# Attention stage of a two-layer kernel: row loads in a hand-written order, the edges' rows moved forward, mixing in four column groups

## The chip, the cores and the metric

One core of one Trainium2 chip runs the whole program. The metric is the time of one execution on the device, in microseconds (us); lower is better. Times are given as the median of several runs, and one more execution was recorded by the hardware profiler. TensorE is called PE here, VectorE DVE, ScalarE ACT, GpSimd POOL and SyncE SP; SPq is SP's queue of transfers.

## The reference, cut to what matters

Two layers on a tensor x of 4 images, 192 channels and 128 x 128 pixels, in float32. The stage in question is the attention of the first:

```
qkv = dwconv3x3(conv1x1(x, w_qkv), w_dw)
q, k, v, l = jnp.split(qkv, 4, axis=1)
q, k, v = (heads(q), heads(k), heads(v))          # b, 8 heads, 24 channels, 128*128
q = q / jnp.maximum(jnp.linalg.norm(q, axis=-1, keepdims=True), EPS)
k = k / jnp.maximum(jnp.linalg.norm(k, axis=-1, keepdims=True), EPS)
attn = jax.nn.softmax(jnp.einsum('bhcn,bhdn->bhcd', q, k) * temperature[None], axis=-1)
out = jnp.einsum('bhcd,bhdn->bhcn', attn, v).reshape(b, c, h, w)
...
out = conv1x1(L + out + x, w_proj) + L
```

The attention is over channels: each head's result is a 24 x 24 matrix for each image. L is a small gate from the mean of l. The second layer adds a depthwise convolution to this output and makes a local attention over 3 x 3 neighbours with dilations 1, 2 and 3.

## The kernel before

The program has three stages.

**Projection** (`project`). It multiplies x with w_qkv and stores the rows of q and k, still without their 3 x 3 convolution, to `qk_dram`, laid out by image row, channel, image and column. It convolves v and stores it. A planner orders the instructions of all engines by costs and due times (`Schedule`, `Stage`); the change doesn't touch it.

**Channel attention** (`channel_attention`, the stage of the change). It goes through 8 heads. A head has 24 channels of q and 24 of k; these 48 channels n are taken in 6 tiles of 8 (in the text, tile 1 to tile 6 of a head; in the code a tile is numbered from 0 over all heads). For each tile:

- a transfer `few` (L705) loads the taps of the vertical filters, and POOL spreads them into a banded matrix `band` (L730, L732): 4 times one large copy and two small ones,
- 16 transfers (L719) load the rows into a buffer u of 2 MB: 32 image rows of two channels each, to 32 partitions. Three buffers take turns: `lent`, which is memory of the last stage, and two of `u_p`,
- PE convolves (`convolve`, L740) with 32 x 32 blocks of `band`, on all sixteen 32 x 32 parts of its array. Each of the 8 channels takes 12 products. The order is such that three channels are in work at a time. ACT copies each result out of PSUM (L749), and DVE gathers its statistics (L751).

Image rows are cut into four strips of 32 rows, so the rows at the three strip edges lack a neighbour. They are mended apart: `cut_loaded` (L775) loads 4 image rows around an edge in 4 transfers (q or k, two halves of the channels), each of 48 partitions with 2 KB; `cut_convolved` (L791) makes their products, `cut_kept` copies them out on ACT, `cut_turned` (L808) transposes them, and `cut_squares` adds them to the squares of the norms.

`products` is the end of a head: the products of edges 0 and 1, then for each of 4 images 128 products `gram` of q with k (L847), between them the turning of an edge and, after the first image, the products of edge 2. `finish` makes the softmax; it is called in pieces while the next head is convolved. `mix` multiplies the 24 x 24 matrices of a head with 24 rows of w_proj (L927) and writes the result into `mix1` and `mix2` by transfers (L931, L934); it is called in two pieces of two images each from the next head's `products`, and its transfers and that of `wph` (L920) are issued by ACT.

**Second pass**: it multiplies x and v with `mix1` and `mix2` and does the second layer. PE, DVE and POOL are busy in it nearly all the time.

What sets the order in the attention: PE's instructions stand as they are written (`tc.manual_schedule`). Those of SP, ACT, DVE and POOL are put in order by the framework's scheduler, from the data they wait for. [...] A transfer that SP or ACT issues also waits until the one eight places before it has landed, since eight semaphores take turns for both queues.

Of the kernel before, what the change touches and what calls it, by code (L numbers as in the profile page):

```python
# [7 lines left out]
F32 = mybir.dt.float32  # L8
# [318 lines left out]
def channel_attention_then_dilated_attention(ctx: ExitStack, tc: tile.TileContext, d, out: bass.AP):  # L327
# [23 lines left out]
    with ExitStack() as early:  # L351
        band_p, u_p = (early.enter_context(tc.tile_pool(name=n, bufs=k)) for n, k in (("pab", 1), ("pau", 2)))
        gate_w = early.enter_context(tc.tile_pool(name="p1g", bufs=1))
        gate_p = early.enter_context(tc.tile_pool(name="p1s", bufs=2))
        sums = []
        for p in range(B // 2):
            xsum = gate_p.tile([128, 3, NB], F32, tag="xsum", name=f"xsum{p}")
            xcol = gate_p.tile([128, 3, 2, H], F32, tag="xcol", name=f"xcol{p}")
            xrow = gate_p.tile([128, 3, 3], F32, tag="xrow", name=f"xrow{p}")
            nc.gpsimd.memset(xrow, 0.0)  # L360
            sums.append((xsum, xcol, xrow))
        later = {}
# [14 lines left out]
        channel_attention(tc, d, load, qk_dram, mix1, mix2, band_p, u_p, gate_p, lent, gates)  # L377
        w2 = {n: later[n] for n in SECOND}
# [291 lines left out]

def channel_attention(tc, d, load, qk_dram, mix1, mix2, band_p, u_p, gate_p, lent, gates):

# [6 lines left out]
    with ExitStack() as ctx:  # L679
# [3 lines left out]
        cut_p = ctx.enter_context(tc.tile_pool(name="pac", bufs=1))  # L683
        few_p = ctx.enter_context(tc.tile_pool(name="pax", bufs=2))
        st = ctx.enter_context(tc.tile_pool(name="pas", bufs=1))
# [3 lines left out]

        bands = [band_p.tile([128, 4, 2, 3, STRIP], F32, tag=f"band{k}", name=f"band{k}") for k in range(2)]  # L690
# [9 lines left out]

        def loaded(hd, which, j):

            c0 = which * C + hd * CH0 + j
            few = few_p.tile([STRIP, 4, 2, 3, STRIP], F32, tag="few", name=f"few{which}_{hd}_{j}")
# [4 lines left out]
            )  # L709
            turn = 3 * (2 * hd + which) + j // 2  # L710
            if turn % 3 == 0:
                u = lent.rearrange("p (e c w) -> p e c w", e=4, c=2)
            else:
                u = u_p.tile([128, 4, 2, B * W], F32, tag="u", name=f"u{which}_{hd}_{j}")
            for e in range(4):
                first = c0 + e * (CH0 // 4)
                for r in range(4):
# [4 lines left out]
                    )  # L722
            if hd and len(bands) == 2:
                for k in range(2):
                    bands.append(gate_p.tile([128, 4, 2, 3, STRIP], F32, tag="xcol", name=f"band{2 + k}"))
                    nc.gpsimd.memset(bands[-1], 0.0)
            band = bands[turn % len(bands)]
            for i in range(4):
                group = slice(i * STRIP, (i + 1) * STRIP)
                nc.gpsimd.tensor_copy(band[group, :, :, :, 1 : STRIP - 1], few[:, :, :, :, 1 : STRIP - 1])  # L730
                for e, m in ((i, 0), ((i + 1) % 4, STRIP - 1)):
                    nc.gpsimd.tensor_copy(band[group, e, :, :, m : m + 1], few[:, e, :, :, m : m + 1])  # L732
            return band, u

# [33 lines left out]

        def cut_loaded(hd, edge, queue):
            u = cut_p.tile([128, 2, B * W], F32, tag=f"u{edge % 2}", name=f"cut{hd}_{edge}")  # L770
            first = (edge + 1) * STRIP - 2
            for which in range(2):
                for h in range(2):
                    c0 = which * C + hd * CH0 + h * (CH0 // 2)
                    queue.dma_start(  # L775
                        u[h * G : h * G + 2 * CH0, which],
                        qk_dram[first : first + 4, c0 : c0 + CH0 // 2].rearrange("r c b w -> r c (b w)"),
                    )
            return u
# [45 lines left out]
        def products(hd, q, sq, k, sk, us, taps):  # L825
            gram = ps_c.tile([128, B, W], F32, tag="pc", name=f"gram{hd}")[:, :, : 2 * CH0]
            cuts, two = [], 2 * CH0
            pcut = cut_convolved(hd, (0, 1), us, taps)
            us[2] = cut_loaded(hd, 2, nc.scalar)
            s_cut = cut_kept(hd, 0, pcut)  # L830
            for b in range(B):
                for v in range(W // 4):
                    if v == W // 8 and b < 2 and mixes:
                        next(mixes[0], None)
                        if b:
                            mixes.pop()
                    if (b, v) == (3, W // 8):
# [48 lines left out]
            by_image = lambda a: a.rearrange("p (b c) -> p b c", b=B)  # L886
            nc.vector.tensor_copy(logits[:, :, hd % 2, :], by_image(sm[:, : B * CH0]))
            nc.vector.tensor_copy(nk[:, :, hd % 2, :], by_image(sm[:, B * CH0 : 2 * B * CH0]))
            nc.vector.tensor_copy(nq[:, :, hd % 2], sm[:, 2 * B * CH0 : EXTRA])

        def finish(hd):


            rows, norm_q, norm_k = logits[:, :, hd % 2, :], nq[:, :, hd % 2], nk[:, :, hd % 2, :]
            wide = lambda a: a.unsqueeze(2).to_broadcast([CH0, B, CH0])
# [16 lines left out]
            nc.vector.tensor_mul(rows, rows, wide(tot))  # L912
            mixes.append(mix(hd))
            next(mixes[-1])

        def mix(hd):

            low = min(max(128 - hd * CH0, 0), CH0)
            wph = fin.tile([CH0, C], F32, tag="wph", name=f"wph{hd}")
            nc.scalar.dma_start(wph, d["wph"][:, hd, :])  # L920
            yield
            for b in range(0, B, 2):
                mixed = fin.tile([CH0, 2, C], F32, tag="mixed", name=f"mixed{hd}_{b}")
                pm = ps_s.tile([128, SM], F32, tag="sm", name=f"pm{hd}_{b}")
                two = pm[:CH0, : 2 * C].rearrange("p (h o) -> p h o", h=2)
                for e in range(2):
                    nc.tensor.matmul(two[:, e, :], logits[:, b + e, hd % 2, :], wph, start=True, stop=True)  # L927
                nc.vector.tensor_copy(mixed, two)
                for e in range(2):
                    if low:  # L930
                        nc.scalar.dma_start(mix1[b + e][hd * CH0 : hd * CH0 + low], mixed[:low, e, :])  # L931
                    if low < CH0:
                        at = G + hd * CH0 + low - 128
                        nc.scalar.dma_start(mix2[b + e][at : at + CH0 - low], mixed[low:, e, :])  # L934
                yield

        pending, mixes = [gate(ps_s) for gate in gates], []

        def step():
            while pending:  # L940
                try:
                    return next(pending[0])
                except StopIteration:
                    pending.pop(0)

        def head(hd):

# [4 lines left out]
            order = sorted((0.75 * n + k, n, dx) for n in range(2 * CH0) for k, dx in enumerate((1, 0, 2)))  # L952
            sources, pcs, sums = {}, {}, []
            for _, n, dx in order:
                which, j, e = n // CH0, n % CH0 // 4, n % 4
                if dx == 1:
                    if n % 8 == 0:
                        sources[n // 8] = loaded(hd, which, j)
                    if n == 40:
                        taps = cut_taps(hd)  # L960
                        us = {edge: cut_loaded(hd, edge, nc.sync) for edge in range(2)}
                    pcs[n] = ps_c.tile([128, B, W], F32, tag="pc", name=f"pc{hd}_{n}")
                convolve(*sources[n // 8], e, j % 2, pcs[n], dx)
# [12 lines left out]
        )  # L976
        with tc.manual_schedule(engines={mybir.EngineType.PE}):
            for hd in range(HEADS0):
                head(hd)
            while pending:  # L980
                step()
            for left in mixes:
                for _ in left:
                    pass

# [643 lines left out]
```

## Time and profile before

| | |
|---|---|
| median of 3 runs | 4297.07 us (4279.99 to 4302.99) |
| profiled execution, its own time | 4289.94 us |
| its span, first to last instruction | 4288.2 us |
| granted clock of PE, mean | 0.972 |
| busy share of PE, DVE, POOL, ACT | 96%, 89%, 79%, 61% |
| first product of the attention, start of the last stage's products | 841.25 us, 1499.57 us |

The profile is one execution. Its page gives the busy time of each engine, the span in 40 slices with a digit for the busy share in tenths and the granted clock of PE (9 is 0.9 or more), and groups of instructions by line: `line engine operation out<-in shape xcount | busy us, mean ns | idle before it, and what ended that`. A timeline row is `start us, us, engine line operation xcount [idle before <- what ended it]`. A row of a stretch gives the stretch, its length, the busy time and number of instructions of PE, PEld (weight loads), DVE, ACT and POOL, then PE's granted clock, the mean busy share of the 16 DMA engines and GB/s. Matmuls overlap, so that PE counts as busy while it works at a low rate.

### The profile page before, as it was taken

What the parts mean: (1) busy time and instruction counts of PE and PEld (TensorE: products, weight loads), DVE (VectorE), ACT (ScalarE), POOL (GpSimd) and SP (SyncE); (2) the same over time, 40 slices, a digit from 0 to 9 for tenths busy, and PEclk for the clock granted to TensorE, in tenths of its full rate; (3) what the DMA queues carried; (4) which work ended last, traced back from release to release, by engine and by line L of the source; (5) the groups of instructions that cost most, each with busy time, mean ns of one, the idle gap of its engine ahead of it and who ended that gap; (6) DMA issues with size and microseconds to landing.
All of it is one profiled execution on the core that took longest, in us unless ns stands there. A gap on an engine that the chain in (4) does not pass through costs nothing.

```text
span 4288.2 us, 79574 instructions
## 1 busy us (share of the span) xinstructions
PE 4115.1 (96%) x28064; PEld 1642.4 (38%) x28064; DVE 3820.6 (89%) x5588; ACT 2627.7 (61%) x4882; POOL 3388.9 (79%) x3411
## 2 busy tenths in 40 slices
PE   8999999799999978999999999999999999999996
PEld 3333333365665522333333333333333333333331
DVE  6999999875576548999999999999999999999996
ACT  6999999743344365565656656556655656656531
POOL 6888888732233226999999999999999999999998
PEclk9999999898899989999999999999999999999997
DMA  8888898666576577656666666655655556555521
GB/s 239 265 270 256 266 287 284 201 184 171 163 191 188 150 160 124 132 125 133 132 127 134 125 132 122 135 129 125 135 126 132 123 135 131 130 132 127 117 47 32
DMA packets 482907, 677.16 MB, mean 158 GB/s; under 512 B 143060, under 2 KB 318304, under 8 KB 482508
## 3 DMA queue, kind: packets, MB, share of 16 engines
q1 hardware_dynamic: 441468, 501.43, 41.6%
q0 software_dynamic: 37888, 166.74, 21.1%
q8 instruction: 223, 3.65, 0.4%
q10 hardware_dynamic: 3152, 3.89, 0.3%
q14 instruction: 176, 1.44, 0.1%
HBM read 278.08 MB, written 201.33 MB: 112 GB/s over the span
## 4 chain that ended last, share of the span: by engine, by line
PE 68%; DVE 14%; DMA 5%; issue 4%; POOL 3%; SPq 3%; ACT 1%; ACTq 0%; POOLq 0%; DVEq 0%
PE sc L1281 9%; PE ex L1403 8%; PE ph L1048 7%; PE pu L427 6%; PE pkv L1202 5%; PE pc L740 5%; DVE term L1409 4%; PE pkv L1205 4%; PE q L1262 4%; PE q L1259 4%; PE pu L432 3%; DVE prod L1270 3%; PE gram L847 2%; POOL acc L1412 2%; SPq L719 2%
## 5 line engine op out<-in xcount | busy, mean ns | idle before, releaser
L1412 POOL TENSOR_TENSOR acc<-acc,term 128x512 f32<-128x512 f32 x1536 | 2034.8, 1330 | 142.1 <-DVE term L1409 55.3
L1409 DVE TENSOR_TENSOR term<-ex,vring 128x512 f32<-128x512 f32 (+2 forms) x1596 | 995.4, 659 | 57.0 <-PE ex L1403 43.4
L1270 DVE TENSOR_TENSOR prod<-q,kring 128x1536 f32<-128x1536 f32 (+1 forms) x600 | 1004.6, 1683 | 20.2 <-PE q L1259 8.8
L504 POOL TENSOR_TENSOR v_True<-v_True,side 128x512 f32<-128x512 f32 (+1 forms) x512 | 643.3, 1268 | 125.8 <-ACT side L493 95.6
L1403 PE MATMUL ex<-e_sb,spread 108*128 108x512 bf16 x1728 | 567.2, 387 | 49.7 <-DVE term L1409 32.4
L481 DVE SCALAR_TENSOR_TENSOR pa<-vboth,dwv,pa 128x1024 f32<-128x1024 f32 (+1 forms) x448 | 574.2, 1282 | 42.2 <-ACT pa L474 14.4
L1215 ACT COPY kring<-pkv 64x512 f32<-64x512 f32 x384 | 223.2, 581 | 417.4 <-PE pkv L1205 411.8
L730 POOL COPY band<-few 32x720 f32<-32x720 f32 x192 | 151.1, 787 | 396.2 <-DMA few<-in_bands 336.1
L1100 DVE SCALAR_TENSOR_TENSOR pa<-hboth,posw,pa 128x1024 f32<-128x1024 f32 (+1 forms) x320 | 407.5, 1273 | 37.0 <-ACT pa L1088 18.1
L1281 PE MATMUL sc<-prod,pick 128*32 128x512 f32 x3456 | 428.8, 598 | 1.7 <-DVE prod L1270 1.7
L1403 PEld LDWEIGHTS <-spread 108*128 108x128 bf16 x1728 | 133.2, 97 | 660.6 <-issue 638.4
L1428 ACT COPY o<-po 128x512 f32<-128x512 f32 x192 | 106.2, 588 | 442.6 <-PE po L1425 237.3
L1048 PE MATMUL ph<-lent,mix 128*64 128x512 f32 (+1 forms) x1024 | 374.1, 596 | 0.6 <-DMA mix<-mixed 0.6
L1202 PE MATMUL pkv<-y,wkv 128*128 128x512 f32 x768 | 364.3, 596 | 9.8 <-DMA y<-moved 9.6
L427 PE MATMUL pu<-xt,wx 128*128 128x512 f32 x768 | 357.2, 608 | 16.8 <-ACT vboth L463 8.9
L493 ACT ACTIVATE side<-ring,dwv 128x512 f32<-128x512 f32 (+1 forms) x512 | 347.8, 724 | 30.1 <-POOL v_True L504 26.3
L1132 ACT ACTIVATE side<-hring,posw 128x512 f32<-128x512 f32 (+1 forms) x512 | 340.9, 710 | 13.0 <-DMA side<-side 11.1
L751 DVE BATCH_NORM_STATS2 stats<-conv 128x6 f32<-128x128 f32 x1536 | 304.4, 274 | 29.2 <-ACT conv L749 26.6
L749 ACT COPY conv<-pc 128x512 f32<-128x512 f32 x384 | 228.7, 616 | 127.6 <-PE pc L740 120.5
L740 PE MATMUL pc<-u,band 32*32 32x508 f32 (+1 forms) x6144 | 276.0, 595 | 4.1 <-DMA u<-qk_dram 1.9
L1215 ACT COPY vring<-pkv 64x512 f32<-64x512 f32 x384 | 223.8, 583 | 45.5 <-PE pkv L1205 32.5
L427 PEld LDWEIGHTS pu<-xt,wx 128*128 128x128 f32 x768 | 142.3, 192 | 222.4 <-issue 121.5
(170 smaller groups left out, 6340.4 us busy)
## 6 DMA issues: line engine op xcount, KB each, us to landing
qk_dram<-us SPq DMA_DIRECT2D x192, 512.0 KB
side<-side POOLq DMA_DIRECT2D x124, 768.0 KB, 7.2
u<-qk_dram SPq DMA_DIRECT2D x512, 128.0 KB
xt<-in_x SPq DMA_DIRECT2D x64, 512.0 KB
v_dram<-v_False SPq DMA_DIRECT2D x64, 512.0 KB
lent<-qk_dram SPq DMA_DIRECT2D x256, 128.0 KB
lent<-in_x SPq DMA_DIRECT2D x128, 256.0 KB
lent<-v_dram SPq DMA_DIRECT2D x128, 256.0 KB
```

The costliest lines, as they stand in the source:

```text
L427: mm(pu, wx[:, mt * 128 : (mt + 1) * 128], tiles["xt", n][:, im, :], start=True, stop=False)
L481: nc.vector.scalar_tensor_tensor(by_row(to[:, o : o + length]), by_row(vboth[:, at : at + length, :, t % 3 : t % 3 + W]), dwv[:, 0, t : t ...
L504: nc.gpsimd.tensor_add(v[:, rows, :], v[:, rows, :], z[:, rows, :])
L740: nc.tensor.matmul(pc[r * STRIP : (r + 1) * STRIP, :, to], band[at, e, c, dx, :], u[at, e, c, :].rearrange("p (b w) -> p b w", w=W)[:, :, of],
L1048: mm(to, w[:, cols], tiles["xv", n, j, im], start=j == 0, stop=j == 2)
L1202: mm(rows3(tile_of("pc", key)), w, tiles["y", n, im], start=True, stop=False)
L1215: nc.scalar.copy(rows[HALVES[im], :, pad : pad + W], rows3(tiles["pkv", n, pair, im])[HALVES[e]])
L1270: nc.vector.tensor_mul(to[:, :, px].rearrange("p t (r w) -> p t r w", w=W), q.unsqueeze(1).to_broadcast([128, 3, *q.shape[1:]]), three,)
L1281: mm(sc[quad * 32 : (quad + 1) * 32, :], pick[:, QR - 4 * row : QR - 4 * row + 32], tiles["prod", n, k // NT, k % NT // 3][:, k % 3, :], s ...
L1403: mm(rows3(tile_of("ex", ("ex", n, g, t))), spread[:, t, :], e_sb, start=True, stop=True)
L1409: nc.vector.tensor_mul(rows3(to[:, px]), rows3(ex[:, px]), win)
L1412: nc.gpsimd.tensor_add(tiles["acc", n, g], tiles["acc", n, g], tiles.pop(("term", n, g, t)))
```

## The change

It has five parts, all in `channel_attention`.

1. SP's order is now written by hand too. `load_rows(t)` loads tile t of the 48 tiles of all heads. Three are loaded ahead of the first head; from then on, tile t + 3 is loaded once tile t has been convolved. All of a tile's 16 transfers and its taps stand together.
2. There are three band matrices, one for each buffer, where there were two in the first head and four in the others; the taps `few` have one buffer instead of two.
3. The taps of the edges and the rows of all three edges (12 transfers) are loaded right after tile 5 of the same head has been asked for (n == 15), all by SP, into three buffers. Before, SP loaded edges 0 and 1 and ACT loaded edge 2 after the products of the first two.
4. The products of edge 2 come right after those of edges 0 and 1, ahead of the first image's `gram`.
5. `mix` is one piece for all 4 images: four products side by side in four column groups of PE, one copy by DVE. The 24 columns of the softmax's matrix are padded to 32 with zeros for that. Its transfers are issued by POOL, and `wph` is loaded by SP.

```
-        bands = [... for k in range(2)]
+        bands = [... for k in range(3)]
...
-        logits = fin.tile([CH0, B, 2, CH0], F32, tag="logits", name="logits")
+        logits = fin.tile([CH0, B, 2, STRIP], F32, tag="logits", name="logits")
+        nc.gpsimd.memset(logits, 0.0)
...
-        def loaded(hd, which, j):
+        def load_rows(t):
+            if t >= 6 * HEADS0:
+                return
+            hd, which, j = t // 6, t // 3 % 2, t % 3 * 2
...
-            band = bands[turn % len(bands)]
+            band = bands[t % 3]
...
-            return band, u
+            sources[t] = band, u
...
-            u = cut_p.tile([128, 2, B * W], F32, tag=f"u{edge % 2}", name=f"cut{hd}_{edge}")
+            u = cut_p.tile([128, 2, B * W], F32, tag=f"u{edge}", name=f"cut{hd}_{edge}")
...
-            pcut = cut_convolved(hd, (0, 1), us, taps)
-            us[2] = cut_loaded(hd, 2, nc.scalar)
+            pcut = {**cut_convolved(hd, (0, 1), us, taps), **cut_convolved(hd, (2,), us, taps)}
...
-                    if v == W // 8 and b < 2 and mixes:
-                        next(mixes[0], None)
-                        if b:
-                            mixes.pop()
+                    if (b, v) == (1, W // 8) and mixes:
+                        mixes.pop()()
...
-                if b == 0:
-                    pcut.update(cut_convolved(hd, (2,), us, taps))
...
+            pm = ps_s.tile([128, SM], F32, tag="sm", name=f"pm{hd}")[:, :C]
+            for b in range(B):
+                mine = slice(b * STRIP, (b + 1) * STRIP)
+                nc.tensor.matmul(pm[mine], logits[:, b, hd % 2, :], wph[hd], start=True, stop=True)
+            mixed = fin.tile([128, C], F32, tag="mixed", name=f"mixed{hd}")
+            nc.vector.tensor_copy(mixed, pm)
+            for b in range(B):
+                first = b * STRIP
+                if low:
+                    nc.gpsimd.dma_start(mix1[b][hd * CH0 : hd * CH0 + low], mixed[first : first + low])
...
+        def load_mixing(hd):
+            wph[hd] = fin.tile([CH0, C], F32, tag="wph", name=f"wph{hd}")
+            nc.sync.dma_start(wph[hd], d["wph"][:, hd, :])
...
-                    if n % 8 == 0:
-                        sources[n // 8] = loaded(hd, which, j)
-                    if n == 40:
-                        taps = cut_taps(hd)
-                        us = {edge: cut_loaded(hd, edge, nc.sync) for edge in range(2)}
...
                 evicted(fulls[which], stats[which], e * (CH0 // 4) + j, pcs.pop(n))
+                if n % 8 == 7:
+                    load_rows(6 * hd + n // 8 + 3)
+                if n == 15:
+                    taps = cut_taps(hd)
+                    us = {edge: cut_loaded(hd, edge) for edge in range(3)}
+                    if hd:
+                        load_mixing(hd - 1)
...
-        with tc.manual_schedule(engines={mybir.EngineType.PE}):
+        sources, wph = {}, {}
+        with tc.manual_schedule(engines={mybir.EngineType.PE, mybir.EngineType.SP}):
+            for t in range(3):
+                load_rows(t)
             for hd in range(HEADS0):
                 head(hd)
+            load_mixing(HEADS0 - 1)
```

More of the change, by code (lines that the diff above doesn't have):

```diff
@@ L376, in channel_attention_then_dilated_attention @@
         ]
-        channel_attention(tc, d, load, qk_dram, mix1, mix2, band_p, u_p, gate_p, lent, gates)
+        channel_attention(tc, d, load, qk_dram, mix1, mix2, band_p, u_p, lent, gates)
         w2 = {n: later[n] for n in SECOND}
@@ L668, in gate_bias, with channel_attention @@
     nc.vector.tensor_copy(bias, pb)
-def channel_attention(tc, d, load, qk_dram, mix1, mix2, band_p, u_p, gate_p, lent, gates):
+def channel_attention(tc, d, load, qk_dram, mix1, mix2, band_p, u_p, lent, gates):
     nc = tc.nc
@@ L683, in channel_attention @@
         cut_p = ctx.enter_context(tc.tile_pool(name="pac", bufs=1))
-        few_p = ctx.enter_context(tc.tile_pool(name="pax", bufs=2))
+        few_p = ctx.enter_context(tc.tile_pool(name="pax", bufs=1))
         st = ctx.enter_context(tc.tile_pool(name="pas", bufs=1))
@@ L688, in channel_attention @@
         ps_s = ctx.enter_context(tc.tile_pool(name="paps", bufs=1, space=bass.MemoryType.PSUM))
-        bands = [band_p.tile([128, 4, 2, 3, STRIP], F32, tag=f"band{k}", name=f"band{k}") for k in range(2)]
+        bands = [band_p.tile([128, 4, 2, 3, STRIP], F32, tag=f"band{k}", name=f"band{k}") for k in range(3)]
         for band in bands:
@@ L709, in loaded @@
             )
-            turn = 3 * (2 * hd + which) + j // 2
-            if turn % 3 == 0:
+            if t % 3 == 0:
                 u = lent.rearrange("p (e c w) -> p e c w", e=4, c=2)
@@ L722, in loaded @@
                     )
[L723 to L726, printed above, removed]
-            band = bands[turn % len(bands)]
+            band = bands[t % 3]
             for i in range(4):
@@ L767, in cut_taps, with cut_loaded @@
             return taps
-        def cut_loaded(hd, edge, queue):
-            u = cut_p.tile([128, 2, B * W], F32, tag=f"u{edge % 2}", name=f"cut{hd}_{edge}")
+        def cut_loaded(hd, edge):
+            u = cut_p.tile([128, 2, B * W], F32, tag=f"u{edge}", name=f"cut{hd}_{edge}")
             first = (edge + 1) * STRIP - 2
@@ L774, in cut_loaded @@
                     c0 = which * C + hd * CH0 + h * (CH0 // 2)
-                    queue.dma_start(
+                    nc.sync.dma_start(
                         u[h * G : h * G + 2 * CH0, which],
@@ L886, in products @@
             by_image = lambda a: a.rearrange("p (b c) -> p b c", b=B)
-            nc.vector.tensor_copy(logits[:, :, hd % 2, :], by_image(sm[:, : B * CH0]))
+            nc.vector.tensor_copy(logits[:, :, hd % 2, :CH0], by_image(sm[:, : B * CH0]))
             nc.vector.tensor_copy(nk[:, :, hd % 2, :], by_image(sm[:, B * CH0 : 2 * B * CH0]))
@@ L891, in finish @@
         def finish(hd):
-            rows, norm_q, norm_k = logits[:, :, hd % 2, :], nq[:, :, hd % 2], nk[:, :, hd % 2, :]
+            rows, norm_q, norm_k = logits[:, :, hd % 2, :CH0], nq[:, :, hd % 2], nk[:, :, hd % 2, :]
             wide = lambda a: a.unsqueeze(2).to_broadcast([CH0, B, CH0])
@@ L912, in finish @@
             nc.vector.tensor_mul(rows, rows, wide(tot))
-            mixes.append(mix(hd))
-            next(mixes[-1])
+            mixes.append(lambda: mix(hd))
         def mix(hd):
             low = min(max(128 - hd * CH0, 0), CH0)
[L919 to L935, printed above, removed]
+            pm = ps_s.tile([128, SM], F32, tag="sm", name=f"pm{hd}")[:, :C]
[8 more added lines that the diff above has]
+                    nc.gpsimd.dma_start(mix1[b][hd * CH0 : hd * CH0 + low], mixed[first : first + low])
+                if low < CH0:
+                    at = G + hd * CH0 + low - 128
+                    nc.gpsimd.dma_start(mix2[b][at : at + CH0 - low], mixed[first + low : first + CH0])
         pending, mixes = [gate(ps_s) for gate in gates], []
@@ L952, in head @@
             order = sorted((0.75 * n + k, n, dx) for n in range(2 * CH0) for k, dx in enumerate((1, 0, 2)))
-            sources, pcs, sums = {}, {}, []
+            pcs, sums = {}, []
             for _, n, dx in order:
@@ L956, in head @@
                 if dx == 1:
-                    if n % 8 == 0:
-                        sources[n // 8] = loaded(hd, which, j)
-                    if n == 40:
-                        taps = cut_taps(hd)
-                        us = {edge: cut_loaded(hd, edge, nc.sync) for edge in range(2)}
                     pcs[n] = ps_c.tile([128, B, W], F32, tag="pc", name=f"pc{hd}_{n}")
-                convolve(*sources[n // 8], e, j % 2, pcs[n], dx)
+                convolve(*sources[6 * hd + n // 8], e, j % 2, pcs[n], dx)
                 if dx != 2:
@@ L982, in channel_attention @@
             for left in mixes:
-                for _ in left:
-                    pass
+                left()
 def second_pass(tc, x, w2, xv_p, mix1, mix2, biases, v_dram, v2_dram, out):
```

## The prediction

> **What bounds the kernel now.** I read the slices of the page first, then the stage's stretches, the waits of PE and SP in it, and last the timelines of one head.
>
> ```profile
> PE   8999999799999978999999999999999999999996
> ...
> PEclk9999999898899989999999999999999999999997
> ```
>
> PE is full almost everywhere. Each slice is 107 us; the granted clock is under 0.9 only between slices 8 and 15, around the channel attention, and in the last. PE's timeline puts that stage between 841.3 and about 1499.6 us. Nothing that the change edits works outside these 658 us, except the loads and fills that it moves across the stage's two ends. So the question is one head, eight times. From PE's timeline the heads start at 841.3, 928.7, 1015.3, 1101.8, 1182.1, 1262.2, 1341.1 and 1417.4: 87.4 us for head 0 and (1499.6 - 928.7) / 7 = 81.6 for the others. Head 3, the SP queue, then PE (start, us, work):
>
> ```profile
> 1128.27 0.37 SPq L705 DMA_DIRECT2D few<-in_bands  x1
> 1128.74 9.25 SPq L719 DMA_DIRECT2D u<-qk_dram  x16
> 1138.04 0.42 SPq L766 DMA_DIRECT2D cuttaps<-in_cuttaps  x1
> 1138.50 5.14 SPq L775 DMA_DIRECT2D cut<-qk_dram  x8
> 1143.74 0.39 SPq L705 DMA_DIRECT2D few<-in_bands  x1
> 1144.24 13.03 SPq L719 DMA_DIRECT2D lent<-qk_dram  x16
> ```
>
> ```profile
> 1145.85 1.06 PE L791 MATMUL pcut<-cut,cuttaps 48*32 48x512 f32 x8
> 1147.81 1.02 PE L791 MATMUL pcut<-cut,cuttaps 48*32 48x512 f32 x2 [0.90 <-DMA cut<-qk_dram]
> 1149.22 7.59 PE L791 MATMUL pcut<-cut,cuttaps 48*32 48x512 f32 x38 [0.39 <-DMA cut<-qk_dram]
> 1156.73 2.80 PE L847 MATMUL gram<-conv,conv 128*48 128x48 f32 x64
> ```
>
> ```profile
> 1140.00:1145.00 5.00, 5.00 (x142) 3.29 (x140) 3.31 (x17) 3.09 (x6) 0.00 (x0) 1.00 0.26 88
> 1145.00:1150.00 5.00, 3.71 (x28) 0.44 (x13) 4.78 (x22) 1.64 (x3) 0.00 (x0) 0.98 0.61 165
> 1150.00:1155.00 5.00, 5.00 (x36) 1.61 (x36) 0.00 (x0) 0.00 (x0) 3.03 (x9) 0.50 0.60 171
> 1155.00:1160.00 5.00, 5.00 (x76) 3.03 (x68) 0.00 (x0) 0.58 (x1) 1.14 (x4) 0.50 0.76 215
> ```
>
> The first two edges' 48 products take 10.9 us here; in head 0, where their rows lay ready, 2.7. PE waits for transfer after transfer, its clock is 0.50 for ten microseconds, and the first products of q and k run at that clock. The last three columns of the stretches (clock, DMA share, GB/s) say why the rows are late: while they move, the share is 0.26. By the semaphore events, the eight transfers of head 3 land at 40.7, 41.7, 42.7, 43.7, 45.8, 47.3, 48.5 and 49.6 us after the head's start: 1.0 us each, then 1.3 on average once the next tile's transfers move too. The filter taps (few) issued behind them land 0.25 us after the eighth: what follows does not overtake.
>
> **The loads, three tiles ahead.** The three u buffers already allow exactly this: SP issues tile t+3 when tile t's products release its buffer (head 3: its fourth tile at 1107.2, 5.4 us after the head's start). From there the loads run without a gap: tiles 4 to 6 of a head are issued 5-15, 15-26 and 26-36 us after its start. The order by hand keeps this pace, so in heads 1 to 7 it is worth nothing, except where it removes ACT's transfers from the ring of eight landings that SP waits for; those waits (for wph, 27.0 us in all) fall into tiles loaded for the next head, which are needed some 10 us later. I cost them at nothing; without that cover head 7 shows the price, its fourth tile 4 us late.
>
> At the start the hand order costs. Before, tiles 2 and 3 were loaded strip by strip during the projection, and the stage began with edges and tile 4:
>
> ```profile
> 841.13 0.34 SPq L511 DMA_DIRECT2D v_dram<-v_False  x1
> ...
> 845.15 0.34 SPq L766 DMA_DIRECT2D cuttaps<-in_cuttaps  x1
> 845.54 5.37 SPq L775 DMA_DIRECT2D cut<-qk_dram  x8
> 851.00 13.38 SPq L719 DMA_DIRECT2D lent<-qk_dram  x16
> ```
>
> In the changed kernel's instruction order only tile 1 stays ahead, its last transfer stands behind the last v store and the small constants, so at 845.15, and all of tiles 2 and 3 follow. With 9.2 us of issue a tile and 0.4 for taps: tile 2 846.0-855.2, tile 3 -865, tile 4 -875.2, tile 5 -885.3, which is 44 us after the start where it was 32. Head 0 ends 12 us later. PE itself begins at 841.25 as before, since it waits for v_False.
>
> **The edges early.** All twelve row transfers now stand behind tile 5 and ahead of tile 6's taps and rows. Tile 5 lands 29.3 us after the head's start (mean of heads 2 to 6). The twelve: first 1.4 us later, seven at 1.0, five at 1.3 (by then tile 6's first transfers move, as in head 3): 29.3 + 1.4 + 6.0 + 6.5 = 43.2. Tile 6's taps land 0.3 later, at 43.5; POOL must spread them before any product of tile 6 can run:
>
> ```profile
> L730 POOL COPY band<-few 32x720 f32<-32x720 f32 x184 | 144.9, 787 | 390.7 <-DMA few<-in_bands 330.9 <-PE pc L740 39.9 <-PE sm L883 11.9
> ...
> L791 PE MATMUL pcut<-cut,cuttaps 48*32 48x508 f32 (+1 forms) x576 | 102.8, 766 | 12.2 <-DMA cut<-qk_dram 12.0
> ...
> L732 POOL COPY band<-few 32x6 f32<-32x6 f32 x368 | 63.4, 198 | 28.4 <-PE pc L740 27.6
> ```
>
> 4 x (787 + 2 x 198) ns = 4.7 us, so 48.2. Tile 6's rows land 8 us behind the edges (as the sixteen lent transfers did in head 3), at 51.2; products end 5.3 us after the last landing (1140.5 to 1145.8 in head 3): 56.5. PE stands idle from 34 to 48.2, so it starts cold. A tile takes 6.5 us warm and took 8.8 in head 0 after a 25 us wait: 48.2 + 8.8 = 57.0, which ends last. Then edges 0 and 1 (2.8), edge 2 (2.7, head 5), 64 + 64 products for the first image (3.1) and the turning (0.7): the second image begins at 66.3. Before it began at 70.6, 68.8, 65.8, 65.7, 64.3, 61.9 and 69.0 in heads 1 to 7, mean 66.6. The rest is 14.5 us (12.3 and 2.2, heads 3 to 7), so a head takes 80.8 instead of 81.6: the ten microseconds at the edges are gone, and tile 6 comes thirteen later, once without and once with the cold clock. Seven heads: -5 us.
>
> [...]
> [...]
>
> **Small parts.** Taps with one buffer: SP waits at few until POOL has spread the last ones; in the loads' pace that is 2 us landing + 4.7 of 9.2, covered, and after the edges 48.2 against SP's own 48: nothing, at most 2 us where POOL is late. Three bands for four: the band of tile t+3 is written after tile t, seven or more microseconds before its use. Mixing: PE had 8 instructions twice, 0.8 us (and 1.1 cold); now once, in four column groups, between 0.3 and 0.8; 0.3 us a head of the part I count, 2 in all. Its four transfers go to POOL, about 1 us each (the nearest row, side, 997 ns), waiting for DVE's copy late in the head; queued behind is a spread for the next head's third tile, needed some 20 us later. wph moves from ACT to SP, 0.4 us in a queue that ends each head 8 us idle. At the end the last mixing saves one copy and gains POOL's issue: between -2 and +2 us, I take -1. Padding logits is a fill before the stage.
>
> **Sum.** 12 - 5 - 2 - 1 = +4 on the profiled execution of 4289.94 (span 4288.2): 4294. The runs' median of 4297.07 is 7 above it: 4301.
>
> **Rivals.** (1, 0.43) The stall is moved: 4301, own range 4281 to 4318, within 0.5% (21 us, about what this measurement can tell from no change). (2, 0.37) Slower: the edges' transfers beside other traffic. The four that ACT issued beside u took 1.4 to 1.8 us each. At 1.5 for all twelve the last lands at 47.2, 4 us later, and everything of the head behind it: 8 x 4 = 32, 4333. For it: tile 6 now competes for the same engines; against: seven run alone. It decides from a mean of 1.35 on. (3, 0.17) Faster: tile 6 overtakes, since most of its data needs the other twelve engines. If it lands 5.5 us earlier, 8 x 5.5 = 44 less: 4257. Against: the taps behind the eighth transfer. (4, 0.03) The hand order leaves the order as it was and only the start counts: 4309; the built order speaks against it.
> Faster 0.18, same 0.45, slower 0.37. The range takes rivals 2 and 3 in: 4262 to 4343.
>
> **What would show it.** Right: pcut 5 to 6 us in one piece without DMA waits; the wait for u or few ahead of the sixth tile over 10 us, with the clock at 0.5 there; head 0 near 99 us; DMA share near 0.3 some 30 us into each head. Wrong: tile 6 starting before the twelfth edge transfer has landed, or heads well off 81 us.

## The result and the profile after

The changed kernel takes 4289.99 us (median of 20 runs, 4284.06 to 4295.95), the kernel before 4293.53 us (median of 20, 4278.47 to 4304.17): a ratio of 0.9994 with a 95% interval of 0.9985 to 1.0002. That is no difference. The forecast was 4301 with a range of 4262 to 4343, and "within 0.5%" its likeliest case.

An equal time does not mean equal work. The page's slices first:

```profile
PE   8999999797887888999999999999999999999996
...
PEclk9999999898998999999999999999999999999997
```

In slices 10 to 14, counted from 1, PE's digit is 8 or 7 where it was 9, so PE is idle more, and the granted clock is under 0.9 in slices 8, 10 and 13 where it was in 8, 10, 11 and 15. In the stretch from 841 to 1500 us PE is busy 557.46 us instead of 627.78, and the stage still lasts 664.5 us (before 658.3). So PE did not work less; before, slow products waiting for their rows had counted as busy (those of the edges 102.8 us, now 42.6). Head 3 of the changed kernel starts at 1095.9 us. SP's queue and then PE (start, us, work):

```profile
1111.67 10.94 SPq L722 DMA_DIRECT2D u<-qk_dram  x16
1122.66 0.42 SPq L765 DMA_DIRECT2D cuttaps<-in_cuttaps  x1
1123.13 7.75 SPq L774 DMA_DIRECT2D cut<-qk_dram  x12
1131.32 0.33 SPq L937 DMA_DIRECT2D wph<-in_wph  x1
1132.32 0.33 SPq L709 DMA_DIRECT2D few<-in_bands  x1
1133.39 10.98 SPq L722 DMA_DIRECT2D u<-qk_dram  x16
```

```profile
1125.97 4.35 PE L739 MATMUL pc<-u,band 32*32 32x512 f32 x114 [0.52 <-DMA u<-qk_dram]
1141.00 13.80 PE L739 MATMUL pc<-u,band 32*32 32x512 f32 x216 [10.68 <-POOL band L731]
1154.74 5.33 PE L790 MATMUL pcut<-cut,cuttaps 48*32 48x512 f32 x72
1160.00 3.08 PE L843 MATMUL gram<-conv,conv 128*48 128x48 f32 x128
```

The twelve edge transfers stand between tile 5 and tile 6, as the change says. The 72 products of the three edges now run in one piece of 5.33 us, where the first 48 alone had taken 10.9, and the wait has moved in front of tile 6: PE stands 10.68 us and is said to wait for POOL's `band`. The same place in the stretches:

```profile
1125.00:1130.00 5.00, 4.49 (x116) 2.16 (x114) 4.61 (x25) 2.45 (x4) 0.00 (x0) 1.00 0.26 93
1130.00:1135.00 5.00, 0.32 (x7) 0.00 (x0) 2.01 (x11) 0.59 (x1) 0.00 (x0) 0.76 0.39 131
1135.00:1140.00 5.00, 0.00 (x0) 0.00 (x0) 0.00 (x0) 0.00 (x0) 0.00 (x0) 0.50 0.55 161
1140.00:1145.00 5.00, 4.00 (x22) 1.05 (x38) 0.00 (x0) 0.00 (x0) 4.16 (x12) 0.50 0.91 238
```

From 1135 to 1140 no engine works. The DMA share is 0.26 while the edges' rows move, the same figure that stood beside the late rows before; by the semaphore events the first of them lands 30.7 us after the head's start, where it was 40.7; the clock has fallen to 0.50 when tile 6 begins. Over the stage, the groups of these lines (count | busy us, mean ns | idle before them, what ended it) and the two waits in front of tile 6 (total us, times, longest):

```profile
L739 PE MATMUL pc<-u,band 32*32 32x508 f32 (+1 forms) x6144 | 299.7, 646 | 87.5 <-POOL band L731 86.5 <-DMA u<-qk_dram 0.9
...
L790 PE MATMUL pcut<-cut,cuttaps 48*32 48x508 f32 (+1 forms) x576 | 42.6, 590 | 0.0
```

```profile
PEld pc L739 <- POOL band L731: 104.2, 17, 13.4
...
PE pc L739 <- POOL band L731: 86.5, 8, 12.5
```

The products of the edges are busy for 60 us less than before (102.8), their 12.2 us of idle time are gone, and 86.5 us of waiting appear at tile 6, eight times. By PE's timeline the heads start at 839.7, 935.9, 1015.0, 1095.9, 1178.7, 1259.9, 1341.4 and 1422.4 us and the last stage at 1504.15: 96.2 us for head 0, and a mean of 81.18 for the others.

### The profile page after: what moved, and what is told of

Read it like the earlier page. It is cut to its first block, busy times and chain, and to the rows that moved or that the text cites. A ratio compares the mean times of both kernels' runs of the same rounds, so it can differ in the third digit from the quotient of the medians.

```text
span 4291.1 us, 79590 instructions
## 1 busy us (share of the span) xinstructions
PE 4050.4 (94%) x28064; PEld 1634.9 (38%) x28064; DVE 3813.2 (89%) x5580; ACT 2629.8 (61%) x4882; POOL 3406.0 (79%) x3447
## 4 chain that ended last, share of the span: by engine, by line
PE 73%; DVE 13%; issue 4%; DMA 4%; SPq 2%; POOL 2%; ACT 1%; DVEq 0%; POOLq 0%; ACTq 0%
PE sc L1279 9%; PE ex L1401 8%; PE ph L1046 8%; PE pu L427 7%; PE pc L739 6%; PE pkv L1200 5%; DVE term L1407 5%; PE pkv L1203 4%; PE q L1260 4%; PE q L1257 4%; PE pu L432 4%; DVE prod L1268 3%; PE gram L843 2%; PE pu L578 2%; PE po L1423 2%
## 5 line engine op out<-in xcount | busy, mean ns | idle before, releaser
L1407 DVE TENSOR_TENSOR term<-ex,vring 128x512 f32<-128x512 f32 (+2 forms) x1596 | 999.7, 663 | 56.5 <-PE ex L1401 43.4
L739 PE MATMUL pc<-u,band 32*32 32x508 f32 (+1 forms) x6144 | 299.7, 646 | 87.5 <-POOL band L731 86.5
L1213 ACT COPY vring<-pkv 64x512 f32<-64x512 f32 x384 | 223.9, 583 | 46.6 <-PE pkv L1203 33.5
L739 PEld LDWEIGHTS pc<-u,band 32*32 32x32 f32 x6144 | 173.4, 107 | 179.0 <-POOL band L731 104.2
```

The costliest lines, as they stand in the source:

```text
L739: nc.tensor.matmul(pc[r * STRIP : (r + 1) * STRIP, :, to], band[at, e, c, dx, :], u[at, e, c, :].rearrange("p (b w) -> p b w", w=W)[:, :, of],
L1213: nc.scalar.copy(rows[HALVES[im], :, pad : pad + W], rows3(tiles["pkv", n, pair, im])[HALVES[e]])
L1407: nc.vector.tensor_mul(rows3(to[:, px]), rows3(ex[:, px]), win)
```

## The experiments

Theory: the zero is two effects that cancel. Asking for all edges' rows together, by SP, and making their products together gains, since the second image no longer waits for ACT's four late transfers; asking for them ahead of tile 6 loses about as much, since tile 6 queues behind them. Rivals: the parts are each worth nothing; or the wait that the profile names, POOL's spreading of the taps, is the loss. Each was run beside the kernel before, whose medians were 4291.8 to 4297.0 us. The head lengths below are means of heads 1 to 6 in one profiled execution each (before 81.45, after 81.09).

**The edges' rows late.** The changed kernel, with one number other:

```
-                if n == 15:
+                if n == 23:
```

> The changed kernel with the edges' rows asked for after tile 6 instead of after tile 5 (n == 23 for n == 15), all else as in the change, rows on four engines. Theory (the stall is only moved): tile 6 starts at 34 to 35 us of the head again, the twelve land by 54, PE waits for them cold, the second image begins near 62 to 66, a head takes 77 to 81 us: 4260 to 4290. If the early place as such were a gain that something else ate up, this one would be slower than the change: over 4310.

Measured: 4246.01 us (4243.2 to 4251.66), ratio 0.9887 (0.9872 to 0.9901). That is more than was expected of it. Heads take 76.09 us. PE's timeline in its head 3 (start 1082.3):

```profile
1119.38 7.22 PE L739 MATMUL pc<-u,band 32*32 32x512 f32 x164 [0.77 <-DMA u<-qk_dram]
1126.52 8.29 PE L790 MATMUL pcut<-cut,cuttaps 48*32 48x512 f32 x54
1135.10 2.75 PE L790 MATMUL pcut<-cut,cuttaps 48*32 48x512 f32 x18 [0.28 <-DMA cut<-qk_dram]
1137.77 3.08 PE L843 MATMUL gram<-conv,conv 128*48 128x48 f32 x128
```

There is no hole ahead of tile 6, and the edges' products take 11.2 us again, since their rows come as they run. Even so the first image starts 55.5 us after the head's start, where the changed kernel started it at 64.1. The early place alone costs 44 us.

**The edges together, and nothing else.** The kernel before, with one taps buffer to make the room:

```
-                        us = {edge: cut_loaded(hd, edge, nc.sync) for edge in range(2)}
+                        us = {edge: cut_loaded(hd, edge, nc.sync) for edge in range(3)}
...
-            pcut = cut_convolved(hd, (0, 1), us, taps)
-            us[2] = cut_loaded(hd, 2, nc.scalar)
+            pcut = {**cut_convolved(hd, (0, 1), us, taps), **cut_convolved(hd, (2,), us, taps)}
```

> The kernel before with one thing alone: the four transfers of edge 2 are asked for by SP right behind those of edges 0 and 1, at the old late place, and the products of the three edges stand together (parts 3 and 4 without the early place; one buffer for the taps makes the room). Theory: this is what the changed kernel gains and the early place gives back; the second image no longer waits for ACT's four transfers, 6 us a head, about 45 us in all: 4245 to 4260. Rival: the gain of the late variant came from the loads by hand three tiles ahead; then this stays at 4285 to 4295.

Measured: 4258.28 us (4252.92 to 4261.81), ratio 0.992 (0.9899 to 0.994). Heads 1 to 6 take 76.49 us, nearly as with the late edges of the changed kernel (76.09): so the gain in a head is the edges' standing together, and the loads by hand add little to it.

The theory's reason is only part of the gain. From the end of the convolution to the second image, heads 1 to 6 take 14.1 to 15.2 us here, and the granted clock stays at 1.00 all the while. In the kernel before, the six of heads 1 to 7 in which the clock fell (mean 0.66 to 0.77 over that stretch) take 20.0 to 26.5 us, but head 6, the one at 1.00, takes 16.7. So, by that one head, about 2 us are gained at the full clock, and they go again into the later end of the convolution (the whole head 6 takes 76.3 us before, no more than the heads here); the rest of the gain goes together with the clock's staying up. Head 7 of this run shows the reverse: there the clock falls, as in the second row here (the first is of head 3), the stretch takes 21.4 us, and the head is 6.6 us longer than the mean of heads 1 to 6. These are readings of one profiled execution each, and why the clock stays up in heads 1 to 6 and falls in head 7 stays open.

```profile
1135.00:1140.00 5.00, 5.00 (x137) 3.74 (x136) 0.55 (x1) 0.00 (x0) 2.97 (x9) 1.00 0.75 207
1447.00:1452.00 5.00, 5.00 (x79) 3.54 (x80) 0.32 (x1) 0.00 (x0) 0.00 (x0) 0.50 0.06 20
```

**More engines for the edges' rows.** A transfer of 4 rows by 12 channels leaves five semaphore events in the trace, one of u sixteen. While the edges' rows move, the share is 0.26 of the 16 DMA engines (1125 to 1130, above), so by estimate they use about 4; while tile 6's rows move it is 0.91 (1140 to 1145), about 15. With channels outermost a transfer of the edges leaves 13 events; as five go with 4 engines, these are taken for 12, an estimate too, since the trace names no engine:

```
-                        qk_dram[first : first + 4, c0 : c0 + CH0 // 2].rearrange("r c b w -> r c (b w)"),
+                        qk_dram[first : first + 4, c0 : c0 + CH0 // 2].rearrange("r c b w -> c r (b w)"),
```

(with the taps in the same order). It was put into the changed kernel, the kernel before, and the changed kernel with late edges:

> The changed kernel, with one edit: the rows of the edges are laid out channel by channel (12 channels x 4 rows) instead of row by row (4 rows x 12 channels), and the edges' taps to match; same bytes, same number of transfers, same packets of 2 KB, same place in SP's queue. Theory (a transfer of 4 x 12 rows runs on 4 of the 16 DMA engines, and the sixth tile queues behind it on those four): with 12 engines the twelve transfers take SP's issue, 12 x 0.64 = 7.7 us, instead of 14; tile 6 begins 5 us earlier in each head, 8 x 5 = 40 less: 4250 us, and a transfer shows 13 semaphore events instead of 5. Rival (they are slow because their packets are small and come from rows far apart, whatever the engines): no change, 4290, landings 1.0 to 1.3 us apart as now.

> The kernel before, with the same edit alone (edges' rows channel by channel). Theory: edges 0 and 1 land as the sixth tile's products end, their products take 3 to 4 us instead of 10, the clock stays up, edge 2 waits some 2 us; a head takes about 70 us instead of 81.6: 8 x 11 = 90 less, 4205 us. Rival (small packets): 4294, no change.

> Both: the changed kernel, edges' rows after tile 6 and channel by channel. Theory: tile 6 ends at 44 us, the twelve are issued at 36 to 44 and land by 47, products of the edges end at 50 and the head at 69 to 72 us, where SP's queue (67 us of issue a head) becomes the bound: 8 x 10 = 80 less than the change, 4210 us. Rival (small packets): as the run with four engines in the same place.

Measured: early 4270.31 us, ratio 0.9941 (0.9926 to 0.9955); before 4254.33, ratio 0.9906 (0.9891 to 0.992); late 4217.57, ratio 0.9821 (0.9805 to 0.9837). All three gain, so the rival of small packets falls, and the first two gain less than expected. In the kernel before, edges 0 and 1 now cost 3 to 4.7 us in heads 1 to 7, but ACT's four transfers for edge 2 still land 54 to 62 us after the head's start. In the early place the rows land every 0.8 us instead of 1.0 to 1.3, and in heads 1 to 7 tile 6's first product comes at 39.8 to 41.1 us instead of 42.4 to 46.3; late, it comes at 32.1 to 36.4. The positions in a head (us from its start, means of heads 1 to 6) show where each kernel gains and loses:

| | convolution ends | second image begins | head |
|---|---|---|---|
| before | 44.3 | 66.2 | 81.45 |
| before, edges together | 46.6 | 61.6 | 76.49 |
| before, 12 engines | 44.7 | 62.8 | 77.48 |
| changed (early) | 57.1 | 66.0 | 81.09 |
| changed, 12 engines | 54.1 | 63.0 | 78.36 |
| changed, late | 44.3 | 61.2 | 76.09 |
| changed, late, 12 engines | 45.8 | 56.5 | 72.05 |

The step to 12 engines gains 20 us in the early place and 28 in the late one, so the few engines are not what makes the early place dear: with 12, it is still 53 us dearer (4270.31 - 4217.57). That is the time of twelve transfers in front of the one tile of the head that has none to spare; late, they stand in front of the next head's first tile, whose products begin some 22 us after the twelfth landing. SP's time for the twelve, in head 3 with 12 engines early and in head 2 with 12 engines late (7.75 us in the changed kernel, above):

```profile
1114.98 9.73 SPq L774 DMA_DIRECT2D cut<-qk_dram  x12
...
1033.80 9.98 SPq L774 DMA_DIRECT2D cut<-qk_dram  x12
```

**Tile 6's taps ahead of the edges' rows.** The profile's largest named wait, taken away:

```
                 if n == 15:
+                    if hd:
+                        fews[6 * hd + 5] = load_taps(6 * hd + 5, gate_p, "xcol")
                     taps = cut_taps(hd)
```

> The changed kernel with tile 6's filter taps asked for ahead of the edges' rows instead of behind them, in heads 1 to 7. Nothing else moves. The profile names POOL's spreading of these taps as the largest wait of PE in the stage: 86.5 us in 8 places and 104.2 us on the weight loads. Theory: the rows of tile 6 stand behind the same twelve transfers and land at 50 to 53 us after the head's start, so the wait passes from POOL to the transfer of u and the tile's convolution still ends about 5 us after that, 55 to 57: 1 to 2 us a head, 4280 to 4290. Rival: the named wait is the limit; the tile can begin at 34 us and most of 80 us goes, 4210 to 4230.

Measured: 4286.58 us, ratio 0.9991 (0.9982 to 0.9999); heads 80.57 us. In heads 1 to 7 the named wait is gone (8.2 us of it are left, in head 0), and in its place stands

```profile
PE pc L746 <- DMA u<-qk_dram: 75.0, 7, 11.6
```

The rival falls: of 86.5 us named, 3.4 came back by the medians and 6.7 by the profiled executions. POOL has spread tile 6's taps by 31.9 to 34.1 us, but its first product still comes at 42.2 to 44.4; the tile's last rows land at 50 to 52 us as before, and its products end 5 us after that.

**The mixing alone** (part 5, in the kernel before):

> The kernel before with part 5 alone: mixing in one piece with four column groups, its transfers on POOL, wph by SP. Theory: part 5 is small, 0.3 us a head on PE and none on the waits, so 4287 to 4295 us against 4293 before, and the 47 us between the kernel before and the changed kernel with late edges come from the edges being asked for together by SP. Rival: ACT's transfers for the mixing hold up the ring of landings and with it u; then this kernel alone is 20 us or more faster, 4275 or less.

Measured: 4295.74 us, ratio 1.0011 (1.0002 to 1.0019), so 4 us slower, if anything; the rival falls. PE's products of the mixing (before, then this run) take 1.6 us a head less:

```profile
L927 PE MATMUL pm<-wph,logits 24*24 24x192 f32 x56 | 15.5, 410 | 0.0
```

```profile
L920 PE MATMUL pm<-wph,logits 24*32 24x192 f32 x56 | 4.2, 376 | 0.0
```

In the length of a head this can't be seen: heads 1 to 7 take 81.27 us against 81.56, but heads 1 to 6 take 81.78 against 81.45, and single heads lie between 76.8 and 88.8. The stage begins 3.5 us later in this execution.

**The start.** The first three tiles' loads put back ahead of the hand order, in the changed kernel, and later in the kernel with late edges on 12 engines:

```
+        for t in range(3):
+            load_rows(t)
         with tc.manual_schedule(engines={mybir.EngineType.PE, mybir.EngineType.SP}):
-            for t in range(3):
-                load_rows(t)
```

> The changed kernel with the loads of the first three tiles put back ahead of the hand-written order, so that they are asked for during the projection, as before. Theory: only head 0 gains, from 96 us back to about 87; 4281 us, ratio 0.998. Rival: head 0 is long because its tile 6 waits for the edges as in every head, and the start adds only 2 or 3 us; then 4287 or more.

> The kernel with the edges' rows late and on 12 engines (4218 us, sixteen transfers a tile), with the first three tiles' loads put back into the projection. By the run of the start alone, head 0 loses 12 us and the stage begins 3 us later: 7 us less in the stage, so about 4211. Rival: the stage is no longer bound where the start showed, and nothing comes of it: 4218.

Measured: 4286.82 us, ratio 0.9988 (0.9979 to 0.9996), and 4215.14 us (4208.57 to 4223.7), ratio 0.9814 (0.9798 to 0.9829). Head 0 gains what was said, 84.2 us instead of 96.2, and 79.7 instead of 86.5; but the stage starts later, at 843.1 instead of 839.7 us, and at 843.4 instead of 837.0. The first run came to its rival's figure (4287) and not to 4281, and the second shows its rival too: nothing that can be measured against 4217.57. In the seven kernels whose first tiles are loaded during the projection the stage starts at 838.4 to 852.0 us (mean 844.1), in the seven others at 836.6 to 839.7. What the loads save in head 0 they take, in part, from the end of the projection.

**Fewer, larger transfers.** In the kernel with late edges on 12 engines SP's waits come to some 48 us in 600, and it was taken that SP's issue is the bound; so a tile's sixteen transfers were joined into seven of the same bytes:

```
-                for r in range(4):
+                for r, rows in ((0, 4 - e), (4 - e, e)):
```

> The changed kernel with the edges' rows late and on 12 engines (4218 us before this run), and with the sixteen transfers of a tile's rows joined into seven, of up to 128 partitions, with the same bytes. Theory: a tile costs SP 9.3 us of issue, a head 6 x 9.7 + 12 x 0.8 = 68 us of the 72 that the head takes, so SP's issue is what bounds now; with seven transfers a tile the head falls to 64 to 66 us and the time to about 4165. Rival: the bytes or PE bound the head, and the time stays within 10 us of 4218.

Measured: 4275.88 us, ratio 0.9967 (0.9952 to 0.9981): 58 us slower than with sixteen, and so neither the forecast nor its rival. SP's waits (total us, times, longest) pointed at the one taps buffer:

```profile
SPq L723 <- PE pc L740: 155.3, 62, 16.3
SPq L709 <- POOL band L732: 132.9, 38, 5.8
```

so a second one was given to it, and in a further run the start of before as well:

> The kernel of the joined transfers again (rows of the edges late and on 12 engines, seven transfers a tile; 4276 us, where sixteen transfers gave 4218), with two buffers for the taps of the tiles instead of one, from head 1 on. In the joined kernel SP stood 133 us at the taps until POOL had spread the last ones, where it stood nowhere with sixteen. Theory: with transfers this large the taps land late behind the tile ahead, POOL spreads for 4.7 us, and the one buffer that the change leaves makes SP wait for that once a tile; with two the loss of 58 us goes and the time is 4218 or less, down to 4165. Rival: the large transfers themselves land late (6 to 8 us each), and the time stays near 4276.

> The same with two buffers for the taps, and the first three tiles' loads put back into the projection. If the start is worth what it was before, 5 us less than the kernel without it; a candidate for the fastest version: 4160 to 4213 us.

Measured: 4294.73 us, ratio 1.0002 (0.9991 to 1.0012), and 4294.35, ratio 1.0007 (0.9996 to 1.0019). That theory falls: SP's wait at the taps shrinks to 15.7 us and the time grows. What PE does in the joined kernel's head 2, and at the same place of the kernel with sixteen:

```profile
1066.53 1.38 PE L844 MATMUL gram<-conv,conv 128*48 128x48 f32 x52
1072.55 0.72 PE L844 MATMUL gram<-conv,conv 128*48 128x48 f32 x12 [4.64 <-issue]
...
1074.25 3.98 PE L844 MATMUL gram<-conv,conv 128*48 128x48 f32 x111
1079.94 0.57 PE L844 MATMUL gram<-conv,conv 128*48 128x48 f32 x17 [1.71 <-issue]
```

```profile
1054.13 1.76 PE L843 MATMUL gram<-conv,conv 128*48 128x48 f32 x64
...
1056.41 3.45 PE L843 MATMUL gram<-conv,conv 128*48 128x48 f32 x128
```

PE stops in the middle of a row of products whose data lies ready, and "issue" says that it waited for nothing that the profile shows. The trace of the queue that carries instructions tells more: it has (q8 of the page: 222 packets, 3.64 MB), on average, one packet of 16 KB for some 255 instructions of PE (weight loads counted), and these packets end at 1071.31 and 1078.61 us, 1.2 and 1.3 us before the two stops end. From 930 to 1420 us the joined kernel has 40 stops of PE over 0.5 us, 78 us in all, and 37 of them, 75 us, end within 1.8 us of such a packet's end; with two taps buffers it is 39 of 41 (78 of 81 us), with sixteen transfers 8 of 11 (8 of 11 us). By chance it would be a third, since a packet comes every 5.7 us. The stops put down to "issue" lie closer still: in the joined kernel all 34 of them (72 us) end 1.2 to 1.7 us after a packet's end, and from each to the next PE has 256 instructions or a multiple of that, to within one, in all 33 cases. The likely reading is that PE stops where one packet's instructions end and waits for the next packet, and that the large transfers make it late, since with sixteen transfers only 4 such stops (3.6 us) are left. The packets themselves are hardly longer than before (1.2 us each), so it would be their start that is late. The joined kernel can have 2.3 MB of rows in flight (eight transfers, seven to a tile of 2 MB) instead of 1 MB. The cause is read off the traces and was not tried apart; whether SP's issue bounds the kernel with sixteen transfers stays open.

## Why the prediction was right

The prediction made its sum on one profiled execution, and the profile after gives each term:

| | foreseen | measured |
|---|---|---|
| start of the stage | 0 | -1.6 (839.7 for 841.3) |
| head 0 | +12 | +8.8 (96.2 for 87.4) |
| heads 1 to 7, with the mixing | -5 and -2 | -2.6 (81.18 for 81.56) |
| after the stage | -1 | -1.6 |
| sum | +4 | +3.0 (span 4291.1 for 4288.2, rounded) |

That the sum comes within 1 us of the measured one is in part luck: head 0 was 3.2 us too long and heads 1 to 7 promised 4.4 us too much, and these cancel. The range, 81 us wide, was made to hold most of the rivals as well, so it is the single terms that show whether the mechanism was right.

- **The edges early.** The mechanism and the sizes held. The twelfth transfer lands 40.8 to 44.5 us after the start in heads 1 to 7 (43.2 foreseen), tile 6's rows at 50.1 to 53.1 (51.2), POOL has spread its taps at 45.8 to 49.7 (48.2), the convolution ends at 55.6 to 60.0 (57.0), and the edges' products take 5.3 us (5.5). One detail differs: the first four products of tile 6 need a quarter of the spread each, so its first comes at 42.4 to 46.3; the clock is 0.50 there and is back at 1.00 only 6.3 to 8.9 us later, with waits for POOL and for rows in between. The signs that it named for itself appear: one piece of pcut, ten microseconds of waiting ahead of tile 6, a DMA share of 0.26 there, head 0 near 99.
- **Its gap.** It set "the ten microseconds at the edges are gone" against "tile 6 comes thirteen later" and put both down to the early place. The runs take them apart: the edges' standing together is worth 5 us a head without any early place, most of it together with a clock that stays up, and the early place by itself costs as much. The sum came out right since it was made of landings. The change without its early place, which the prediction did not weigh, measures 44 us lower.
- **Rival 2** (a cadence from 1.35 us on): in head 3 the twelve landings span 12.8 us, 1.16 each. It did not come.
- **Rival 3** (tile 6 overtakes): every start of tile 6 lies after the twelfth landing. With the taps moved out of the way it gained 1 us a head, so the taps were not what held it; the rows were. (Its 4257 lay outside the range of 4262 to 4343 that was said to take it in.)
- **The engines of the edges' rows.** That tile 6 competes for these rows' engines (rival 2) or needs the other twelve (rival 3) no run shows, since no trace names a transfer's engines; what they show is five semaphore events against 13 with 12 channels outermost, and a share of 0.26 while these rows move. The loss doesn't hang on their number: 12 engines, by the estimate above, gain 20 us early and 28 late, and the early place costs 44 us on 4 and 53 on 12. The rows' place in the queue makes the loss.
- **Head 0.** Near in size by luck, not by its parts. Tile 5 starts 4.6 us later than before, not 12, its rows landing 9.5 later; the twelve transfers then hold tile 6, whose first product comes 13.2 later, and the convolution ends 18.2 later; 7.7 us come back up to the second image, which no longer waits for ACT's rows of edge 2, and 1.7 behind it. That head 0 also loses and gains at the edges was not in its 12.
- **Small parts.** The mixing's 0.3 us a head can't be told from the spread of the heads; its transfers cost POOL 0.52 us each where 1 was taken. One taps buffer costs nothing at this pace, as said (SP waits 0.2 us for it in the stage).
- **Heads 1 to 7.** The two terms together were worth 2.6 us and not 7. The second image begins at 66.4 us on average, as foreseen (66.3; before 66.6). But the sum added 14.5 us for the rest of a head, a mean of heads 3 to 7, and compared with 81.6, a mean of heads 1 to 7 in which the rest is 15.0; measured after the change it is 14.8. So some 0.5 us a head of the foreseen gain, 3 us in all, came from the two means and not from the change.
- **The level.** Of the 11 us between 4301 and 4290, the base makes 3.5: the median before was 4297.07 in three runs and 4293.53 in twenty. The rest, 7.5 us, is the difference between one profiled execution and the medians: by the medians the change gains 3.5 us, within the noise, where the profiled executions lose 3.

The fastest version found is the changed kernel with its edges' rows late and on 12 engines: 4217.57 us, and 4215.14 with the start of before, 1.8% below the kernel before and 1.7% below the changed one.

## What to carry over

Ahead of moving a transfer forward, list for each load behind it in the queue how long it has until it is needed: here the twelve edge transfers held up hardly a product of the next head when its tiles stood behind them, and cost 5 us a head in front of the one tile that was already late. When a change gives no difference, run its parts singly before believing that it does nothing: here one was worth about 35 us and another cost 44. Look at the granted clock in each repetition of a loop: here the same stretch of a head took 16.7 us at 1.00 and 20.0 us or more where the clock fell. A wait that names one engine (POOL's band, 86.5 us) can hide a transfer that ends some 4 us after POOL's work, so ask what else the waiting instruction needs before mending what is named.

## What the runs showed of the hardware beside

- The same 96 KB, in transfers that leave 13 events instead of five, landed every 0.8 us instead of every 1.0 to 1.3, but each took SP 0.8 us to issue (9.73 us for twelve) instead of 0.64 (7.75), so the landings kept the pace of the issue.
- Joining transfers took SP's time for a tile's rows from about 9.4 to 4.5 us, and made the kernel 58 us slower; half of the transfers then landed 6.2 to 8.4 us after their issue, where it had been 3.1 to 4.1.
